# A gather split over five queues: number loads for two chunks at once, sums cleared by transfers, and more columns on ACT

## The chip, the cores and the metric

The kernel runs on one core of a Trainium2 chip. The core has TensorE (PE, with its weight loads PEld), VectorE (DVE), ScalarE (ACT), GpSimd (POOL) and SyncE (SP), each with an instruction queue of its own; SP issues transfers only. The metric is the device time of one execution in microseconds, given as the median of three runs. The profile is that of one more execution.

## The reference

One layer of a graph network over 12,500 nodes and 400,000 edges. Edges are sorted by their target `dst`; the sources `src` are random.

```
h    = max(layernorm(x), 0)                              # 12500 x 48
tmp  = [h[dst], h[src], edge_attr]                       # 400000 x (48+48+32)
msg  = relu(tmp @ W1 + b1) @ W2 + b2
out  = x + segment_sum(msg, dst)                         # 12500 x 48
```

Targets follow a square law (`12500 * u ** 2`), so one edge's target is near the next one's, while each edge needs a row of its own for its source.

## The kernel before

**Tables.** The product with W1 is split in three. Two tables are made first: `tab_a` = h @ W1's first 48 rows + b1, for targets, and `tab_b` = h @ W1's next 48 rows, for sources, both in HBM with 128 numbers a node. `bt` is the second table once more, transposed, in SBUF: 128 partitions, one column of four bytes a node.

**Chunks.** The edges go in 391 chunks of 8 tiles of 128 edges (the last has 5). For chunk c the loop in `windows` (lines 501 to 553) works in three iterations. In iteration c, `prepare` loads the edge attributes (`lhs`), the targets (`row`) and 80 consecutive rows of `tab_a` from the chunk's first target on (`rhs`, whose start is a number in a register); DVE turns targets into a one-hot matrix in `lhs` (L379) and later into its transpose `hot` (L389). In iteration c + 1, `before` puts the target part and the edge part into `pre` with 16 PE instructions (L400), `gathered` adds the source part (L421) and `hidden` applies the relu on ACT (`hid`, L437). In iteration c + 2, `fold` sums the messages by target into `p_g` (L445, L448), and `add` puts these 80 columns into a running window `seg` of sums, on DVE (L460).

**Sources: three ways.** A tile of 128 source rows comes to `gathered` in one of three ways.

- POOL gathers a tile with one indirect transfer from `tab_b` (`gb`, L371). Seven `gb` buffers let it work ahead.
- By columns: DVE and ACT copy single columns of `bt` into a tile `gt` (L348), one instruction an edge, its place in a register. Per chunk 143 columns are copied, 71 by DVE and 72 by ACT, so a tile is full about every 0.9 chunks.
- By rows: SP issues one transfer of 512 bytes an edge from `tab_b` (`gs`, L289), 15 per chunk.

`tiles_of` works out which tile of which chunk comes by columns (430 tiles) and by rows (45); POOL has the remaining 2,618.

**Registers.** Places come into registers by a load on the engine's own queue (`numbers`, L272). `PARTS` lists the groups: (by DVE?, place in the strip of numbers, how many). A group is one load, its size rounded up to a multiple of four, and then its copies. DVE has five groups (8, 15, 16, 20, 12; the second load also brings the place for `add`), ACT has six (12, 8, 8, 20, 12, 12). SP loads the chunk's first target and 15 rows' places, 16 numbers a chunk.

**Order.** It is written out by hand (L501 to L553); each engine follows its own instructions in that order. DVE, in an iteration: one-hot (L379), groups 0 and 1, the segment's output add (L495, when there is one), `add` (L460), the segment change (when there is one), group 2, `hot` (L389), groups 3 and 4. ACT: groups 5 to 7, `hid`, groups 8 to 10. PE: `before`, `fold`, `gathered`. SP: `lhs`, `row`, its load of numbers, `rhs`, the rows, then a segment's load or store. SP's transfers take turns at eight completion semaphores, so an issue also waits until the transfer eight places before it has landed. `lhs` and `row` have three buffers each.

**Segments.** Twelve chunks share one window `seg` of 1,024 targets, in two copies. At the end of a segment (`segment_next`, L471) DVE clears the other copy with two memsets (L476), all but its first 80 columns, and carries the last 80 columns over (L478). In the next segment's first chunks PE multiplies the old window by W2 (`segment_sum`, L484), DVE adds it to x (L495), and in the third chunk SP stores it (L499); before that store SP waits for DVE's add.

Of the kernel before, what the change touches and what calls it, by code (L numbers as in the profile page):

```python
# [16 lines left out]
P = 128  # L17
# [7 lines left out]
NCH = (NT + T - 1) // T  # L25
W = 80
# [4 lines left out]
L = 1024  # L31
# [4 lines left out]
STORE = 2  # L36
# [19 lines left out]
ROWS0 = 3  # L56
# [1 line left out]


PARTS = (  # L60
    (True, 0, 8), (True, 8, 15), (True, 24, 16), (True, 40, 20), (True, 60, 12),
    (False, 72, 12), (False, 84, 8), (False, 92, 8), (False, 100, 20), (False, 120, 12),
    (False, 132, 12),
)
PLACE = 23
STRIP = 144
PART = sum(n for _, _, n in PARTS)
SLOT = [at + k for _, at, n in PARTS for k in range(n)]
FIRST_OF = [sum(n for _, _, n in PARTS[:k]) for k in range(len(PARTS))]
RPART = 15  # L70
BASE = 0

BT0 = 16512
SEG0 = 161696
SEG_SIZE = 8 * L


AT_PLACE, AT_SEG, SEG, NEXT = 16, 17, 18, 19
WIDTH = 20
SLOTS = (NCH + 2 + P - 1) // P  # L80
BANK = 4

# [145 lines left out]


def windows(nc, tc, gp, bt, ident, idx, raw, rhss, x_t, tab_a, tab_b, dst, edge_t, w2s, b2s,  # L230
            sources, out_t):


    srci, rel, bw, wrow, last, cols, degs = idx
# [1 line left out]
    with ExitStack() as es:  # L236
        seg = es.enter_context(tc.tile_pool(name="segs", bufs=1))

        segs = [seg.tile([P, 2, L], F32, name=f"seg{k}") for k in range(2)]
# [19 lines left out]
        st = {}  # L259
        gts = {}  # L260
        gss = {}

        def group(c):

# [5 lines left out]
        def numbers(c, at, n, engine, table=last):  # L270

            return nc.values_load_multi_w_load_instructions(  # L272
                table[c % P : c % P + 1, c // P, at : at + n],
                engines=[engine], min_val=0, max_val=1 << 23,
                skip_runtime_bounds_check_because="numbers of nodes, and what is made of them",
            )[1]
# [73 lines left out]
        def prepare(c):  # L350
            n = min(T, NT - c * T)
            at = c * CE
            lhs = ld.tile([P, CE], F32, name="lhs")
            nc.sync.dma_start(lhs[W:K, : n * P], edge_t[:, at : at + n * P])
            row = ld.tile([W, CE], I16, name="row")
            nc.sync.dma_start(
                row[:, : n * P],
                dst[at : at + n * P].rearrange("(o e) -> o e", o=1).to_broadcast([W, n * P]),
            )
            m = max(0, min(RPART, len(BYROWS) * P - (c - ROWS0) * RPART)) if c >= ROWS0 else 0  # L360
            base, *nodes = numbers(c, BASE, 1 + m, mybir.EngineType.SP)
            rhs = rhss[c % 3]
            base = base.with_bounds(min_val=0, max_val=4 * HID * (N - 1))
            nc.sync.dma_start(
                rhs.bitcast(U8)[:W, :],
                taba8[bass.ds(base, 4 * HID * W)].rearrange("(w h) -> w h", w=W),
            )
            st[c] = dict(n=n, rows=nodes)
            gb = gp.tile([P, T, HID], F32, name="gb") if c >= RAW else None
            for t in range(n - len(COLS_OF.get(c, ())) - (c in BYROWS) if c >= RAW else 0):  # L370
                nc.gpsimd.indirect_dma_start(  # L371
                    out=gb[:, t, :], out_offset=None, in_=tab_b[:, :],
                    in_offset=bass.IndirectOffsetOnAxis(
                        ap=srci[:, c * T + t : c * T + t + 1], axis=0
                    ),
                )

            deg = degs[c % 3]
            nc.vector.tensor_scalar(  # L379
                lhs[:W, : n * P], row[:, : n * P], bw[:, c : c + 1], None,  # L380
                op0=ALU.is_equal, op1=ALU.add, accum_out=deg[:, :1],
            )
            st[c].update(rhs=rhs, lhs=lhs, gb=gb, deg=deg)
# [49 lines left out]
        def hidden(c):  # L433
            s = st[c]
            n = s["n"]
            h = wp.tile([P, T, HID], F32, name="hid")
            nc.scalar.activation(h[:, :n, :], s["pre"][:, :n, :], AF.Relu)  # L437
            s["h"] = h
# [32 lines left out]
        def segment_next(g):  # L471

            old, new = segs[g % 2], segs[(g + 1) % 2]
            if g > 0:
                for k in range(2):
                    nc.vector.memset(new[:, k, W:], 0.0)  # L476
            of, = numbers(begin(g), NEXT, 1, mybir.EngineType.DVE)
            nc.vector.tensor_copy(  # L478
                new[:, :, :W], old[:, :, bass.ds(of.with_bounds(min_val=0, max_val=FAR), W)]
            )  # L480

        sums = []
# [18 lines left out]
        with tc.manual_schedule():  # L501
            for c in range(NCH + 2):
                g, k = group(c - 2)
                if c < NCH:
                    prepare(c)
                    rows(c, st[c].pop("rows"))
                if 0 <= c - 1 < NCH:
                    before(c - 1)
                if 0 <= c - 2 < NCH:
                    fold(c - 2)  # L510
                columns(c, 0)
                columns(c, 1)
                segment_add()
                if 0 <= c - 2 < NCH:
                    add(c - 2)
                    if k == GQ - 1:
                        segment_next(g)
                columns(c, 2)
                if c < NCH:
                    compare(c)  # L520
                if c < 2:
                    nc.vector.memset(segs[c], 0.0)
                columns(c, 3)
                columns(c, 4)
                columns(c, 5)
                columns(c, 6)
                columns(c, 7)
                if 0 <= c - 1 < NCH:
                    gathered(c - 1)
                    hidden(c - 1)  # L530
                columns(c, 8)
                columns(c, 9)
                columns(c, 10)
                if k == GQ - 3 or c == NCH - 1:
                    segment_load(g)
                if g > 0 and k < L // BLK:
                    segment_sum(g - 1, k, BLK)
                if g > 0 and k == STORE:
                    segment_store(g - 1, L)
                if c == NCH + 1:  # L540
                    segment_sum(g, 0, END_L)
                    segment_add()
                    segment_store(g, END_L)
                if c < RAW:
                    raw_turn(c)
                if c == 1:
                    sources()
                for i in range(c * TURNS, min((c + 1) * TURNS, BLOCKS)):
                    turn(i)

                if c < PIECES:
                    s = slice(c * PIECE, (c + 1) * PIECE)
                    nc.sync.dma_start(out_t[:, s], x_t[:, s])  # L553
# [126 lines left out]
def tile_gnn_preln(  # L680
# [13 lines left out]
    places: bass.AP,  # L694
    edge_t: bass.AP,
    ones: bass.AP,
    w1: bass.AP,
    b1: bass.AP,
    w2: bass.AP,
# [10 lines left out]
    nc = tc.nc  # L710
# [39 lines left out]
    with tc.tile_pool(name="keep", bufs=1) as keep, tc.tile_pool(  # L750
# [69 lines left out]
        def check():  # L820

            p_c = ps_c.tile([1, P], F32, name="p_c")
            nc.tensor.transpose(p_c, furthest, ident)
            out_of = keep.tile([1, 1], F32, name="out_of")
            nc.vector.tensor_reduce(out_of, p_c, AX.X, ALU.max)
            nc.vector.tensor_scalar(flag, out_of, 0.5, None, op0=ALU.is_gt)

            nc.vector.tensor_scalar_add(wcol, wcol, -HALF)
            nc.vector.tensor_scalar(bw, b0f[:W, :], wcol[:W, :], None, op0=ALU.add)

            nc.vector.tensor_scalar(cols, cols, 4, BT0, op0=ALU.mult, op1=ALU.add)
            rows_at = slice(BASE, BASE + 1 + RPART)
            nc.vector.tensor_scalar(
                last[:, :, rows_at], last[:, :, rows_at], 4 * HID, None, op0=ALU.mult
            )
            nc.vector.tensor_tensor(
                last[:, :, NEXT : NEXT + 1], last[:, :, NEXT : NEXT + 1],
                last[:, :, SEG : SEG + 1], op=ALU.subtract,
            )
            at = last[:, :, AT_PLACE : AT_PLACE + 1]  # L840
            nc.vector.scalar_tensor_tensor(
                at, last[:, :, AT_SEG : AT_SEG + 1], -4.0, at, op0=ALU.mult, op1=ALU.add
            )
            at_place = slice(PLACE, PLACE + 1)
            nc.vector.scalar_tensor_tensor(
                cols[:, :, at_place], cols[:, :, at_place], 1.0, at, op0=ALU.mult, op1=ALU.add
            )
# [5 lines left out]

    with tc.If(outside == 0) as cmp:
        windows(nc, tc, gp, bt, ident, (srci, rel, bw, wrow, last, cols, degs), (xg, wb, ht), rhss,
                x_t, tab_a, tab_b, dst16, edge_t, w2s, b2s, sources, out_t)
    with cmp.Else():
        general(nc, tc, bt, ident, x_t, tab_a, tab_b, src_it, dst_it, dst, edge_t, w1, w2s, b2s,
                accs, out_t)
# [75 lines left out]
```

## Time and profile before

| | us |
|---|---|
| median of three runs | 3365.4 (3362.72 to 3370.66) |
| profiled execution | 3372.65 |
| its span, first to last instruction | 3370.8 |
| ACT busy | 3035.6 (90%) |
| DVE busy | 2800.1 (83%) |
| PE busy | 2775.6 (82%) |
| POOL busy | 2530.0 (75%) |
| DMA engines busy, after the start | about a third |

The span is the time from the first to the last instruction; the profiled execution's own time lies 1.9 us above it. Busy time counts an engine's datapath. Loads into registers, semaphore waits and the issuing of transfers do not count, so a queue can be full while its engine looks idle: such idle time stands as "issue". Rows with a q behind the engine's name (DVEq, ACTq, SPq) are instructions of the queue itself. A group's row gives busy time and mean duration, then the idle time before it and what ended it; copies follow each other before the last has ended, so their mean is longer than their pitch.

### The profile page before, as it was taken

The page shows a single profiled execution, that of the slowest core. Times are in us where ns is not written, and L with a number is a line of the kernel's source. Part 1 is how long each engine was busy: PE and PEld are TensorE (multiplying, and loading weights), DVE is VectorE, ACT ScalarE, POOL GpSimd, SP SyncE. Part 2 cuts the span into 40 slices and gives each one's busy share as a digit, 9 for nine tenths or more (in the row PEclk, how much of TensorE's full clock was granted, in tenths as well). Part 3 has the DMA queues.
Part 4 walks back from the last instruction along what each step waited for, and adds up shares of the span by engine and source line. Part 5 has one row for each costly group of instructions (what it writes and reads, how often), then busy time and mean ns, then how long its engine had stood idle before and what let it go on. Part 6 is the DMA issues. An engine that isn't in the chain of part 4 may idle for free.

```text
span 3370.8 us, 115212 instructions
## 1 busy us (share of the span) xinstructions
PE 2775.6 (82%) x16394; PEld 2158.3 (64%) x16394; DVE 2800.1 (83%) x29140; ACT 3035.6 (90%) x28179; POOL 2530.0 (75%) x2670
## 2 busy tenths in 40 slices
PE   7987778888888888888887788888788788788777
PEld 6666666666666666666666666676666666666565
DVE  6588888888888888888888888888888888888876
ACT  5799998999998999998899999889998999999987
POOL 7677777777777777777777777777777777777776
PEclk9999998998898998988889999888998999899989
DMA  7433333333333333333333333333333333333333
GB/s 262 122 97 104 100 97 100 99 101 100 100 99 100 95 100 102 100 101 97 100 98 101 100 100 102 95 101 97 102 99 98 97 100 98 104 100 97 99 96 83
DMA packets 200234, 349.24 MB, mean 104 GB/s; under 512 B 69219, under 2 KB 107749, under 8 KB 198181
## 3 DMA queue, kind: packets, MB, share of 16 engines
q0 software_dynamic: 84800, 172.53, 18.9%
q1 hardware_dynamic: 114258, 169.09, 16.7%
q14 instruction: 634, 5.19, 0.5%
q8 instruction: 138, 2.26, 0.3%
q10 hardware_dynamic: 404, 0.17, 0.0%
HBM read 322.05 MB, written 22.07 MB: 102 GB/s over the span
## 4 chain that ended last, share of the span: by engine, by line
DVE 71%; issue 14%; PE 5%; DVEq 4%; POOL 2%; DMA 2%; ACT 0%; SPq 0%; POOLq 0%; ACTq 0%
DVE gt L348 47%; DVE lhs L379 12%; DVE hot L389 8%; DVEq L272 4%; DVE seg L460 2%; POOL gb L371 2%; PE pre L400 1%; PE p_g L445 1%; DVE xseg L495 1%; DVE seg L476 1%; DMA row<-in_dst 1%; PE p_f L488 1%; PE p_f L489 1%; DMA gb<-tab_b,srci 1%; PE p_n L195 1%
## 5 line engine op out<-in xcount | busy, mean ns | idle before, releaser
L371 POOL DMA_INDIRECT gb<-tab_b,srci x2618 | 2489.4, 951 | 812.7 <-issue 724.4
L348 ACT COPY gt<-bt 128x1 f32 x27705 | 2618.0, 188 | 63.9 <-issue 54.6
L348 DVE COPY gt<-bt 128x1 f32 x27335 | 1842.1, 144 | 463.3 <-issue 435.1
L400 PEld LDWEIGHTS pre<-rhs,lhs 112*128 112x128 f32 x6250 | 823.5, 208 | 277.1 <-issue 193.4
L400 PE MATMUL pre<-rhs,lhs 112*128 112x128 f32 x6250 | 841.5, 292 | 98.3 <-issue 56.7
L445 PE MATMUL p_g<-hot,hid 128*128 128x80 f32 x6250 | 794.0, 282 | 131.2 <-ACT hid L437 129.1
L445 PEld LDWEIGHTS p_g<-hot,hid 128*128 128x128 f32 x6250 | 758.4, 198 | 164.4 <-ACT hid L437 161.6
L421 PE MATMUL pre<-gb,ident 128*128 128x512 f32 (+2 forms) x1548 | 771.2, 627 | 34.3 <-DMA gb<-tab_b,srci 26.5
L437 ACT ACTIVATE hid<-pre 128x1024 f32<-128x1024 f32 x391 | 397.5, 1017 | 220.2 <-PE pre L421 205.8
L379 DVE TENSOR_SCALAR_CACHE_REDUCE lhs<-row,bw 80x1024 f32<-80x1024 int16 x391 | 494.6, 1265 | 14.8 <-DMA row<-in_dst 14.5
L421 PEld LDWEIGHTS pre<-gb,ident 128*128 128x128 f32 x1548 | 311.8, 225 | 281.0 <-issue 261.7
L421 PE MATMUL pre<-ident,gt 128*128 128x128 f32 x860 | 214.9, 336 | 261.7 <-DVE gt L348 234.7
L421 PEld LDWEIGHTS pre<-ident,gt 128*128 128x128 f32 x860 | 143.8, 210 | 291.5 <-issue 136.4
L389 DVE TENSOR_TENSOR hot<-wnum,rel 128x640 f32<-128x640 f32 x391 | 318.2, 814 | 0.0
L460 DVE TENSOR_TENSOR seg<-seg,p_g 128x160 f32 x391 | 121.5, 311 | 47.8 <-PE p_g L448 47.8
L448 PE MATMUL p_g<-ident,deg 80*128 80x80 f32 x782 | 156.4, 283 | 0.0
L448 PEld LDWEIGHTS p_g<-ident,deg 80*128 80x128 f32 x782 | 123.6, 198 | 0.0
L488 PE MATMUL p_f<-seg,w2s 128*48 128x512 f32 (+1 forms) x134 | 82.2, 700 | 44.3 <-DVE xseg L495 43.9
L489 PE MATMUL p_f<-seg,b2s 1*48 1x512 f32 (+1 forms) x134 | 76.2, 650 | 0.0
L488 PEld LDWEIGHTS p_f<-seg,w2s 128*48 128x48 f32 x134 | 12.3, 135 | 85.9 <-DVE xseg L495 60.0
L476 DVE MEMSET seg<- 128x944 f32 x64 | 54.1, 845 | 9.3
L489 PEld LDWEIGHTS p_f<-seg,b2s 1*48 1x48 f32 x134 | 11.3, 122 | 65.2 <-issue 65.2
(76 smaller groups left out, 429.0 us busy)
## 6 DMA issues: line engine op xcount, KB each, us to landing
gs<-tab_b SPq DMA_DIRECT2D x5760, 0.5 KB
row<-in_dst SPq DMA_DIRECT2D x390, 160.0 KB
lhs<-in_edge_t SPq DMA_DIRECT2D x390, 128.0 KB
gb<-tab_b,srci POOLq DMA_INDIRECT x2618
rhs<-tab_a SPq DMA_DIRECT2D x391, 40.0 KB
xseg<-in_x_t SPq DMA_DIRECT2D x33, 192.0 KB
out_x<-xseg SPq DMA_DIRECT2D x33, 192.0 KB
tab_b<-tab SPq DMA_DIRECT2D x3, 1280.0 KB
```

Of the source, the lines that this page charges most:

```text
L272: return nc.values_load_multi_w_load_instructions(table[c % P : c % P + 1, c // P, at : at + n], engines=[engine], min_val=0, max_val=1 << 23,
L348: copy(gts[j][:, e : e + 1], bt8[:, bass.ds(of, 4)].bitcast(F32))
L371: nc.gpsimd.indirect_dma_start(out=gb[:, t, :], out_offset=None, in_=tab_b[:, :], in_offset=bass.IndirectOffsetOnAxis(ap=srci[:, c * T + t ...
L379: nc.vector.tensor_scalar(lhs[:W, : n * P], row[:, : n * P], bw[:, c : c + 1], None, op0=ALU.is_equal, op1=ALU.add, accum_out=deg[:, :1],)
L389: nc.vector.tensor_tensor(hot[:, :n, :], wnum.unsqueeze(1).to_broadcast([P, n, W]), rel[:, c * T : c * T + n].unsqueeze(2).to_broadcast([P ...
L400: nc.tensor.matmul(pre[:, t, :], s["lhs"][:K, t * P : (t + 1) * P], s["rhs"][:K, :], start=t % BANK == 0, stop=False, skip_group_check=True,)
L421: nc.tensor.matmul(pre[:, t:e, :], lhsT, rhs, start=False, stop=True, skip_group_check=True)
L437: nc.scalar.activation(h[:, :n, :], s["pre"][:, :n, :], AF.Relu)
L445: nc.tensor.matmul(p_g[:, 0, :], s["h"][:, t, :], s["hot"][:, t, :], start=t == 0, stop=t == n - 1)
L448: nc.tensor.matmul(p_g[:, 1, :], s["deg"], ident[:W, :W], start=True, stop=True)
L460: nc.vector.tensor_add(to, to, s["p_g"])
L488: nc.tensor.matmul(p_f[:, :n], w2s, seg[:, 0, s], start=True, stop=False)
```

## The change

- SP loads numbers for two chunks at once, 32 places in every second chunk, and eight first targets in every eighth. It copies 16 rows a chunk.
- The two memsets of the segment change are gone. A new `segment_clear` clears one eighth of the old window by a transfer from a small array of zeros, in each of eight chunks, the third to the tenth of the next segment. SP issues it at the end of its iteration.
- DVE copies 72 columns in four groups (23, 16, 17, 16) and ACT 76 in five (12, 16, 20, 12, 16). The first group's load has 24 numbers and brings the place for `add`. In DVE's order: one-hot, group 0, `add`, group 1, `hot`, groups 2 and 3. ACT: groups 4 and 5, `hid`, groups 6 to 8.
- With 148 columns and 16 rows a chunk, 445 tiles come by columns and 48 by rows; POOL has 2,600.

```diff
 PARTS = (
-    (True, 0, 8), (True, 8, 15), (True, 24, 16), (True, 40, 20), (True, 60, 12),
-    (False, 72, 12), (False, 84, 8), (False, 92, 8), (False, 100, 20), (False, 120, 12),
-    (False, 132, 12),
+    (True, 0, 23), (True, 24, 16), (True, 40, 17), (True, 60, 16),
+    (False, 76, 12), (False, 88, 16), (False, 104, 20), (False, 124, 12), (False, 136, 16),
 )
 PLACE = 23
-STRIP = 144
+STRIP = 152
...
-RPART = 15
-BASE = 0
+RPART = 16
+BASE, BASES = 2 * RPART, 8
+CLEAR = 8
...
-            base, *nodes = numbers(c, BASE, 1 + m, mybir.EngineType.SP)
+            if c % BASES == 0:
+                bases[:] = numbers(c, BASE, BASES, mybir.EngineType.SP)
+            if c % 2 == 0 and c + 1 >= ROWS0:
+                ahead[:] = numbers(c, 0, 2 * RPART, mybir.EngineType.SP)
+            base, nodes = bases[c % BASES], ahead[c % 2 * RPART :][:m]
...
         def segment_next(g):
 
             old, new = segs[g % 2], segs[(g + 1) % 2]
-            if g > 0:
-                for k in range(2):
-                    nc.vector.memset(new[:, k, W:], 0.0)
             of, = numbers(begin(g), NEXT, 1, mybir.EngineType.DVE)
...
+        def segment_clear(g, k):
+
+            n = 2 * (L - W) // CLEAR
+            half, at = divmod(k, CLEAR // 2)
+            nc.sync.dma_start(
+                segs[g % 2][:, half, W + at * n : W + (at + 1) * n],
+                zeros.unsqueeze(0).to_broadcast([P, n]),
             )
...
                 columns(c, 0)
-                columns(c, 1)
                 segment_add()
                 if 0 <= c - 2 < NCH:
                     add(c - 2)
                     if k == GQ - 1:
                         segment_next(g)
-                columns(c, 2)
+                columns(c, 1)
                 if c < NCH:
                     compare(c)
                 if c < 2:
                     nc.vector.memset(segs[c], 0.0)
+                columns(c, 2)
                 columns(c, 3)
                 columns(c, 4)
                 columns(c, 5)
-                columns(c, 6)
-                columns(c, 7)
                 if 0 <= c - 1 < NCH:
                     gathered(c - 1)
                     hidden(c - 1)
+                columns(c, 6)
+                columns(c, 7)
                 columns(c, 8)
-                columns(c, 9)
-                columns(c, 10)
...
+                if g > 0 and begin(g + 1) < NCH and 0 <= k - STORE < CLEAR:
+                    segment_clear(g - 1, k - STORE)
```

What is left out lays out the arrays of numbers on the host in the new order, hands `zeros` through, and widens the range that is scaled once at the start.

More of the change, by code (lines that the diff above doesn't have):

```diff
@@ L69 @@
 FIRST_OF = [sum(n for _, _, n in PARTS[:k]) for k in range(len(PARTS))]
-RPART = 15
-BASE = 0
+RPART = 16
+BASE, BASES = 2 * RPART, 8
+CLEAR = 8
 BT0 = 16512
-SEG0 = 161696
+SEG0 = 162208
 SEG_SIZE = 8 * L
-AT_PLACE, AT_SEG, SEG, NEXT = 16, 17, 18, 19
-WIDTH = 20
+AT_PLACE, AT_SEG, SEG, NEXT = 40, 41, 42, 43
+WIDTH = 44
 SLOTS = (NCH + 2 + P - 1) // P
@@ L230, in windows @@
 def windows(nc, tc, gp, bt, ident, idx, raw, rhss, x_t, tab_a, tab_b, dst, edge_t, w2s, b2s,
-            sources, out_t):
+            zeros, sources, out_t):
     srci, rel, bw, wrow, last, cols, degs = idx
@@ L261, in windows @@
         gss = {}
+        bases, ahead = [], []
         def group(c):
@@ L479, in segment_next @@
                 new[:, :, :W], old[:, :, bass.ds(of.with_bounds(min_val=0, max_val=FAR), W)]
+            )
+        def segment_clear(g, k):
[4 more added lines that the diff above has]
+                zeros.unsqueeze(0).to_broadcast([P, n]),
             )
@@ L696, in tile_gnn_preln @@
     ones: bass.AP,
+    zeros: bass.AP,
     w1: bass.AP,
@@ L831, in check @@
             nc.vector.tensor_scalar(cols, cols, 4, BT0, op0=ALU.mult, op1=ALU.add)
-            rows_at = slice(BASE, BASE + 1 + RPART)
+            rows_at = slice(0, BASE + BASES)
             nc.vector.tensor_scalar(
@@ L855, in tile_gnn_preln @@
         windows(nc, tc, gp, bt, ident, (srci, rel, bw, wrow, last, cols, degs), (xg, wb, ht), rhss,
-                x_t, tab_a, tab_b, dst16, edge_t, w2s, b2s, sources, out_t)
+                x_t, tab_a, tab_b, dst16, edge_t, w2s, b2s, zeros, sources, out_t)
     with cmp.Else():
@@ L883 @@
     numbers[2 : NCH + 2, AT_PLACE] = SEG0 + of % 2 * SEG_SIZE - BT0
-    numbers[:NCH, BASE] = first
+    bases = np.pad(first, (0, -NCH % BASES)).reshape(-1, BASES)
+    numbers[: len(bases) * BASES : BASES, BASE : BASE + BASES] = bases
     numbers[:NCH, SEG] = seg
@@ L895 @@
     rows = by_tile[in_rows].reshape(-1)
-    rows = np.pad(rows, (0, -len(rows) % RPART)).reshape(-1, RPART)
-    numbers[ROWS0 : ROWS0 + len(rows), BASE + 1 : BASE + 1 + RPART] = rows
+    by_chunk = np.zeros((NCH + NCH % 2) * RPART, np.int32)
+    by_chunk[ROWS0 * RPART : ROWS0 * RPART + len(rows)] = rows
+    numbers[: NCH + NCH % 2 : 2, : 2 * RPART] = by_chunk.reshape(-1, 2 * RPART)
     last = np.ascontiguousarray(numbers.reshape(SLOTS, P, WIDTH).transpose(1, 0, 2))
@@ L919 @@
         "ones": np.ones((1, NR // 2 * P), np.float32),
+        "zeros": np.zeros(2 * (L - W) // CLEAR, np.float32),
         "w1": np.asarray(L0_gnn_W1),
```

## The prediction

> **What bounds the kernel now.** First the page: span, busy shares, the gathers.
>
> ```profile
> span 3370.8 us, 115212 instructions
> PE 2775.6 (82%) x16394; PEld 2158.3 (64%) x16394; DVE 2800.1 (83%) x29140; ACT 3035.6 (90%) x28179; POOL 2530.0 (75%) x2670
> L371 POOL DMA_INDIRECT gb<-tab_b,srci x2618 | 2489.4, 951 | 812.7 <-issue 724.4 <-DMA gb<-tab_b,srci 45.5 <-PE pre L421 29.4
> ```
>
> No engine looks full. Next, the busy time by window (500 to 2900 us): of the gathers (L371), then of the one ACT instruction per chunk (L437).
>
> ```profile
> 500.00:2900.00 2400.00, 1816.87 (x1912) 0.90 0.36 99
> 500.00:2900.00 2400.00, 291.95 (x287) 0.90 0.36 99
> ```
>
> A gather takes 2400/1912 = 1.255 us with the gap behind it, so POOL is full without looking it; a chunk takes 2400/287 = 8.36 us. POOL would need (8 - 143/128 - 15/128) x 1.255 = 8.49 us per chunk: it is living off the lead that seven gb buffers gave it at the start. What sets 8.36? DVE's waits, then one of its chunks in order of time, and the register loads (L272) on its queue in that chunk, taken window by window.
>
> ```profile
> DVE gt L348 <- issue: 435.1, 1272, 1.2
> DVE lhs L379 <- DMA row<-in_dst: 14.5, 7, 7.7
> ```
>
> ```profile
> 1509.83 1.28 DVE L379 TENSOR_SCALAR_CACHE_REDUCE lhs<-row,bw 80x1024 f32<-80x1024 int16 x1
> 1512.02 1.00 DVE L348 COPY gt<-bt 128x1 f32 x15 [0.42 <-issue]
> 1512.94 0.31 DVE L460 TENSOR_TENSOR seg<-seg,p_g 128x160 f32 x1
> 1513.78 1.06 DVE L348 COPY gt<-bt 128x1 f32 x16 [0.52 <-issue]
> 1514.76 0.81 DVE L389 TENSOR_TENSOR hot<-wnum,rel 128x640 f32<-128x640 f32 x1
> 1515.76 1.30 DVE L348 COPY gt<-bt 128x1 f32 x20 [0.19 <-issue]
> ```
>
> ```profile
> L272 DVEq TENSOR_LOAD <-cols x1: 605/605/605, 1509.9 to 1509.9; - x1
> L272 DVEq TENSOR_LOAD <-cols x1: 1115/1115/1115, 1510.8 to 1510.8; - x1
> L272 DVEq TENSOR_LOAD <-cols x1: 1114/1114/1114, 1512.6 to 1512.6; - x1
> L272 DVEq TENSOR_LOAD <-cols x1: 1379/1379/1379, 1514.3 to 1514.3; - x1
> L272 DVEq TENSOR_LOAD <-cols x1: 851/851/851, 1516.4 to 1516.4; - x1
> L272 DVEq TENSOR_LOAD <-cols x1: 616/616/616, 1517.8 to 1517.8; - x1
> ```
>
> The loads carry 8, 16, 16, 20 and 12 numbers. From the first to the next chunk's first is 7.9 us, of which they take 605 + 1115 + 1114 + 1379 + 851 = 5064 ns; the other 2.8 us issue 71 copies and three larger instructions. DVE's queue is never free, and nearly all idle time of its datapath is "issue", hardly any a wait for data. So DVE's issuing bounds the loop, not its copying: an ordinary chunk is worth what its loads and issues add up to.
>
> **The change part by part: DVE.** A load costs 605 ns for 8 numbers and 1379 for 20, so 64.5 per number and 89 for the load itself. The four new loads carry 24, 16, 20 (17 rounded up to fours) and 16: 1637 + 1115 + 1379 + 1115 = 5246 ns, 182 more than now, since five numbers more are bought for one load less. Issue: after the 20-number load 0.7 us pass until the next (1514.3 + 1.4 to 1516.4), after the 8-number one 0.3, some 0.03 per copy and 0.06 per group. One copy more and one group less give -0.03. That is +0.15 us per chunk. Above it lies a full queue: when the 851 ns load starts at 1516.4, of 20 copies issued some ten have begun (0.062 us each from 1515.76), so ten stand ahead. A group of 23 would run past ten, and its last copies would issue at the datapath's 0.062: +0.1 at most, none if the queue is longer. I take +0.18 for both, between 0.12 and 0.25.
>
> Against it stand the memsets. First the chunk that has them, then their group.
>
> ```profile
> 3343.64 0.31 DVE L460 TENSOR_TENSOR seg<-seg,p_g 128x160 f32 x1
> 3344.10 1.83 DVE L476 MEMSET seg<- 128x944 f32 x2
> 3346.91 0.81 DVE L389 TENSOR_TENSOR hot<-wnum,rel 128x640 f32<-128x640 f32 x1
> L476 DVE MEMSET seg<- x64: 845/845/845, 225.6 to 3345.1; 128x944 f32 x64
> L272 DVEq TENSOR_LOAD <-last x33: 303/314/545, 125.8 to 3343.7; - x33
> ```
>
> From add to compare it is 3.27 us here and 1.82 in the chunk above: 1.45 for the segment change. The copy of 80 columns stays with its own load (0.31) and issue, and during the memsets the queue ran ahead, which shortens what follows. The saving lies between 0.4 and 1.1; I take 0.7, times 32 pairs. The first and last memset give the segment: (3345.1 - 1 - 225.6)/31 = 100.6 us for 12 chunks. DVE's segment becomes 100.6 + 12 x 0.18 - 0.7 = 102.1 (101.0 to 103.2).
>
> **ACT.** One chunk, and loads of 8 and of 20 numbers:
>
> ```profile
> 1513.64 1.01 ACT L437 ACTIVATE hid<-pre 128x1024 f32<-128x1024 f32 x1
> 1514.55 6.75 ACT L348 COPY gt<-bt 128x1 f32 x72
> 1521.59 1.02 ACT L437 ACTIVATE hid<-pre 128x1024 f32<-128x1024 f32 x1 [0.28 <-PE pre L421]
> L272 ACTq TENSOR_LOAD <-cols x1: 553/553/553, 1511.2 to 1511.2; - x1
> L272 ACTq TENSOR_LOAD <-cols x1: 1263/1263/1263, 1513.2 to 1513.2; - x1
> ```
>
> A copy takes 6.75/72 = 0.094 us, four more cost 0.375 per chunk. Without its wait the cycle is 7.67, so 8.04 after. All 72 ran without a gap: their loads hide behind queued copies. The two new loads of 16 take 1.03 (59 ns a number); ten queued copies cover 0.94 of it. So 8.1, at most 8.4 if the cover is smaller, 97 to 101 us a segment: ACT's slack is nearly used, and a late hid delays PE's fold, then DVE's add.
>
> [...]
>
> **SP.** Its waits at the store (500 to 3000 us), one of its chunks, its loads, and two 128-row transfers of the start:
>
> ```profile
> SPq L499 <- DVE seg L460: 102.6, 17, 10.3
> SPq L499 <- DVE xseg L495: 50.7, 8, 9.2
> 1571.15 0.33 SPq L354 DMA_DIRECT2D lhs<-in_edge_t  x1
> 1573.72 4.81 SPq L289 DMA_DIRECT2D gs<-tab_b  x15
> 1578.64 0.33 SPq L354 DMA_DIRECT2D lhs<-in_edge_t  x1
> L272 SPq TENSOR_LOAD <-last x459: 274/1186/1317, 75.8 to 3363.4; - x153
> 7.99 0.42 SPq L768 DMA_DIRECT2D b0f<-in_first_f  x1
> 9.44 0.93 SPq L771 DMA_DIRECT2D cols<-in_src_strip  x1
> ```
>
> SP's chunk is 7.49 us. Its only real slack is the wait before a store, 153.3 us in 2500/100.6 = 24.9 segments: 6.2 us each. Per segment the change adds: 12 row copies at 4.81/15 = 0.32, +3.8; loads of 32 in six chunks (1186 + 16 x 61 = 2162 ns) for 16 in twelve, with 0.06 around each, -1.6; one and a half loads of eight bases, +1.0; eight clears at 0.42 to 0.93 and 0.05 around, +3.8 to +7.8, likelier the low end, which is also a broadcast to 128 partitions. Odd chunks have no load between the row transfer and the row copies, so a transfer slot is wanted back about 1.2 us sooner; bounds 0 and 0.3 each, +0 to +1.8. Sum +7.0 to +12.8; I take 8.4, so 100.6 + 8.4 - 6.2 = 102.8 (101.4 to 107.2). Behind a clear wait the next chunk's lhs and row transfers, and behind the row transfer DVE's first instruction.
>
> **POOL** is relieved of 18 tiles (15 from columns, 3 from rows): 18 x 1.255 = 22.6 us, worth that only where POOL ends last. That is so near the end:
>
> ```profile
> PE pre L421 <- DMA gb<-tab_b,srci: 26.5, 19, 2.8
> ```
>
> (waits from 2900 us on). The gain is 0 to 26; I take 5, as PE has slack before DVE. Initial loads are wider by 8 and 24 columns: under 1 us.
>
> **The sum.** Three queues end near 102 us per segment; the slowest, SP, is taken: +2.2 x 32 segments = +70, less 5: span 3436. The profiled execution took 3372.65 around its span of 3370.8, the median 3365.4, 5.4 below that span: 3430.
>
> **The rivals.** (1) DVE sets the pace and SP stays inside its slack: clears at 0.42, no slot waits, ACT's loads covered. The segment grows by 12 x 0.15 - 0.7 = 1.1, or 0.7 to 1.5: 3382 to 3408. For it: SP's low end is only 0.8 over its present slack.
>
> (2) Faster: dropping a load saves a fixed time on DVE's queue, and merging 8 and 16 numbers into 24 costs less than the sum. Were 0.4 us saved per chunk, the loop would fall to 8.0, under POOL's (8 - 148/128 - 16/128) x 1.255 = 8.43; POOL would run end to end and the run would lose its 22.6 us: 3343. It decides from about 0.15 saved per chunk. Against it: the four sizes lie on one line with only 89 ns of intercept, and one number alone takes 314. For it: no load of 24 stands in this trace.
>
> [...]
>
> (3) Clears near 0.93, or rows landing behind them: SP's segment over 104.5, above 3490, up to 3570 at the upper bound.
>
> **How the numbers follow.** Issuing with SP at the edge, 3408 to 3490: 0.48. DVE alone, 3382 to 3408: 0.25. Worse: 0.09. Within 0.2%, 3359 to 3372 (a measurement of this kernel tells no less than 0.2%): 0.04. Faster: 0.14. The range 3360 to 3490 leaves out the faster case and the worst; the likeliest one's own range is 3408 to 3490. Slower has 0.48 + 0.25 + 0.09 = 0.82.
>
> **What would show it.** DVE: loads of about 1640 ns, no memsets, more "issue" per chunk although there is a load less. SP: waits at the store near nothing, row waits of DVE above 14.5 us, clears of 0.4 to 0.5. ACT: gaps in its 76 copies ahead of the 16-number loads. POOL: 2600 gathers, more waits for free buffers. The prediction is wrong if the load of 24 costs under 1.3 us, or if the segment, from one seg copy (L478) to the next, is below 100.6.

## The result: 7% slower, and the profile after

The changed kernel takes 3602.2 us (median of four runs, 3600.7 to 3607.0) where the kernel before takes 3367.3 on the same chip: 1.070 times as long, 95% interval 1.068 to 1.072. That is 235 us more, beyond the upper end of the range. The page's span, gathers and chain of the changed kernel:

```profile
span 3599.8 us, 117642 instructions
PE 2893.5 (80%) x16430; PEld 2241.7 (62%) x16430; DVE 2784.2 (77%) x29461; ACT 3240.1 (90%) x29714; POOL 2494.3 (69%) x2652
DVE 24%; SPq 19%; PE 14%; DMA 13%; issue 12%; ACT 10%; POOL 5%; DVEq 2%; ACTq 1%; POOLq 0%
L376 POOL DMA_INDIRECT gb<-tab_b,srci x2600 | 2453.2, 944 | 1032.0 <-issue 727.0
```

Busy shares again name no culprit. The chain does: SP's queue (19%) and transfers (13%) stand on it. In the chain of the kernel before, DVE had 71% and both of these next to nothing:

```profile
DVE 71%; issue 14%; PE 5%; DVEq 4%; POOL 2%; DMA 2%; ACT 0%; SPq 0%; POOLq 0%; ACTq 0%
```

One row gives the segment, the unit of everything below: the copy of 80 columns, once a segment, 33 times. Before, then after (line, count, durations, first and last start):

```profile
L478 DVE COPY seg<-seg x33: 177/179/244, 126.3 to 3345.8; 128x160 f32 x33
```

```profile
L480 DVE COPY seg<-seg x33: 243/245/388, 126.6 to 3574.5; 128x160 f32 x33
```

(3345.8 - 126.3)/32 = 100.61 us before, (3574.5 - 126.6)/32 = 107.75 after. 32 segments of 7.14 more are 228 of the 229 us between the two spans: the loss is inside the loop.

Next the waits of SP's own queue. The columns are total us, times, longest:

```profile
SPq L290 <- DMA lhs<-in_edge_t: 60.3, 100, 2.1
SPq L290 <- DMA seg<-in_zeros: 51.5, 87, 1.7
SPq L510 <- DVE seg L465: 41.7, 22, 7.6
SPq L510 <- DVE xseg L506: 40.4, 12, 29.9
SPq L290 <- DMA row<-in_dst: 32.3, 87, 1.2
```

Before, the two waits at the store (L499 there) came to 153 + 82 us and stood first, and the row copies hardly waited for a transfer slot. After, the waits at the store (L510) are 82 us, and the row copies (L290) wait 144 us for `lhs`, a clear or `row` to land, because these hold the slots they want. SP has become the longest queue. Its order in time shows where the wait sits:

```profile
1505.03 2.49 SPq L290 DMA_DIRECT2D gs<-tab_b  x8
1507.57 0.36 SPq L488 DMA_DIRECT2D seg<-in_zeros  x1
1508.04 0.36 SPq L355 DMA_DIRECT2D lhs<-in_edge_t  x1
1508.46 0.41 SPq L357 DMA_DIRECT2D row<-in_dst  x1
1508.96 0.38 SPq L369 DMA_DIRECT2D rhs<-tab_a  x1
1509.43 7.08 SPq L290 DMA_DIRECT2D gs<-tab_b  x16
...
1518.67 0.41 SPq L357 DMA_DIRECT2D row<-in_dst  x1
1521.70 0.33 SPq L369 DMA_DIRECT2D rhs<-tab_a  x1
1522.13 0.93 SPq L290 DMA_DIRECT2D gs<-tab_b  x3
```

Three copies take 0.93 and eight 2.49, so sixteen would take about 5.0; here they take 7.08. This is a chunk without a load of numbers (nothing between `row` and `rhs`; in the next chunk 3.03 us lie there). The fifth copy wants the slot of the clear, eight transfers back, 3.2 us after its issue, and just finds it free; the sixth waits 1.15 us for that of `lhs`, the seventh 0.47 for that of `row`.

DVE then waits for its rows, and POOL for buffers that PE gives back late:

```profile
POOL gb L376 <- PE pre L426: 264.2, 136, 13.9
DVE lhs L384 <- DMA row<-in_dst: 103.3, 121, 8.7
ACT gt L349 <- issue: 78.9, 254, 0.8
DVE gt L349 <- issue: 590.7, 1326, 1.4
```

Before, the first was 29.4 us in 51 waits, the second 14.5 in 7, the third 54.6 and the last 435.1. So the named waits for rows are less than half of DVE's loss. Its "issue" grew too, and no run splits what of that follows from a late row.

The packet records say how late. Median from SP's issue of a transfer to the end of its last packet, in us, here with three experiments told below:

| | before | after | `late` | `apart` | `narrow` |
|---|---|---|---|---|---|
| `lhs` | 1.73 | 2.62 | 1.73 | 1.85 | 1.77 |
| `row` | 2.59 | 3.10 | 2.60 | 2.74 | 2.59 |
| a clear | | 3.02 | 3.18 | 1.85 | 1.36 |

The changed kernel holds its own comparison: between 500 and 3000 us `lhs` lands in 2.91 us right behind a clear and in 1.78 in the chunks without one, `row` in 3.37 and 2.53.

### The profile page after: what moved, and what is told of

The parts are those of the page before. It is cut to its first block, busy times and chain, and to the rows that moved or that the text cites. A ratio compares the mean times of both kernels' runs of the same rounds, so it can differ in the third digit from the quotient of the medians.

```text
span 3599.8 us, 117642 instructions
## 1 busy us (share of the span) xinstructions
PE 2893.5 (80%) x16430; PEld 2241.7 (62%) x16430; DVE 2784.2 (77%) x29461; ACT 3240.1 (90%) x29714; POOL 2494.3 (69%) x2652
## 4 chain that ended last, share of the span: by engine, by line
DVE 24%; SPq 19%; PE 14%; DMA 13%; issue 12%; ACT 10%; POOL 5%; DVEq 2%; ACTq 1%; POOLq 0%
DVE gt L349 15%; SPq L290 10%; ACT gt L349 9%; DMA row<-in_dst 8%; PE pre L426 5%; DVE lhs L384 4%; PE pre L405 4%; SPq L273 4%; POOL gb L376 4%; DVE hot L394 2%; DMA rhs<-tab_a 2%; PE p_g L450 2%; SPq L355 2%; DVEq L273 2%; DMA gb<-tab_b,srci 1%
## 5 line engine op out<-in xcount | busy, mean ns | idle before, releaser
L376 POOL DMA_INDIRECT gb<-tab_b,srci x2600 | 2453.2, 944 | 1032.0 <-issue 727.0
L349 ACT COPY gt<-bt 128x1 f32 x29240 | 2825.7, 187 | 122.4 <-issue 78.9
L405 PEld LDWEIGHTS pre<-rhs,lhs 112*128 112x128 f32 x6250 | 842.7, 212 | 303.4 <-issue 225.4
L405 PE MATMUL pre<-rhs,lhs 112*128 112x128 f32 x6250 | 860.7, 296 | 114.4 <-DVE lhs L384 69.2
L450 PE MATMUL p_g<-hot,hid 128*128 128x80 f32 x6250 | 816.6, 287 | 167.4 <-ACT hid L442 166.6
L450 PEld LDWEIGHTS p_g<-hot,hid 128*128 128x128 f32 x6250 | 780.4, 203 | 200.3 <-ACT hid L442 198.8
L426 PE MATMUL pre<-gb,ident 128*128 128x512 f32 (+2 forms) x1548 | 810.7, 657 | 0.0
L426 PE MATMUL pre<-ident,gt 128*128 128x128 f32 x890 | 236.1, 355 | 366.9 <-DVE gt L349 301.3
L426 PEld LDWEIGHTS pre<-gb,ident 128*128 128x128 f32 x1548 | 333.7, 239 | 259.5 <-issue 233.5
L499 PE MATMUL p_f<-seg,w2s 128*48 128x512 f32 (+1 forms) x134 | 86.3, 732 | 31.6 <-DVE xseg L506 31.1
L499 PEld LDWEIGHTS p_f<-seg,w2s 128*48 128x48 f32 x134 | 12.4, 136 | 73.4 <-DVE xseg L506 45.2
L506 DVE TENSOR_TENSOR xseg<-xseg,p_f 48x512 f32<-48x512 f32 (+1 forms) x67 | 44.7, 667 | 6.9 <-PE p_f L500 6.9
```

The source lines that it names most:

```text
L349: copy(gts[j][:, e : e + 1], bt8[:, bass.ds(of, 4)].bitcast(F32))
L376: nc.gpsimd.indirect_dma_start(out=gb[:, t, :], out_offset=None, in_=tab_b[:, :], in_offset=bass.IndirectOffsetOnAxis(ap=srci[:, c * T + t ...
L405: nc.tensor.matmul(pre[:, t, :], s["lhs"][:K, t * P : (t + 1) * P], s["rhs"][:K, :], start=t % BANK == 0, stop=False, skip_group_check=True,)
L426: nc.tensor.matmul(pre[:, t:e, :], lhsT, rhs, start=False, stop=True, skip_group_check=True)
L450: nc.tensor.matmul(p_g[:, 0, :], s["h"][:, t, :], s["hot"][:, t, :], start=t == 0, stop=t == n - 1)
```

## The experiments

All ratios are against the kernel before on the same chip, timed in the same batch; times are medians. Segments come from the copy's row, as above.

**Which part costs it.** The theory: SP's queue is now the longest, because of the clears. First, the clears are taken out of the changed kernel and the memsets put back.

```diff
+            if g > 0:
+                for k in range(2):
+                    nc.vector.memset(new[:, k, W:], 0.0)
...
-                if g > 0 and begin(g + 1) < NCH and 0 <= k - STORE < CLEAR:
-                    segment_clear(g - 1, k - STORE)
```

> The changed kernel with the two memsets of the segment change back on DVE and no clears by transfers; all else as changed. Theory S (SP's queue sets the pace, and most of its extra time comes from the clears: their issue, 8 x 0.46 us a segment, and the waits for transfer slots behind them, 5.2 us a segment): SP's work per segment falls from 106.6 to about 97.7 us, DVE's issuing takes over, 3400 to 3430 us where the kernel before takes 3365. Rival R (the 16th row and the paired loads of numbers are what SP cannot bear): above 3520 us. Rival C (the column groups on DVE and ACT set the pace): above 3550.

```profile
DVE 53%; ACT 21%; issue 13%; PE 5%; POOL 3%; DVEq 3%; ACTq 1%; DMA 1%; POOLq 0%; SPq 0%
L483 DVE COPY seg<-seg x33: 173/179/243, 127.0 to 3391.9; 128x160 f32 x33
```

3433.3 us, ratio 1.020 (1.018 to 1.021), 3 us above the range; the trace is of its fastest run, 3419.3, with a segment of 102.03. SP is off the chain. So inside the change, clears in place of memsets cost 3602 - 3433 = 169 us. This is a net figure: the run without clears pays for its memsets.

Then each part alone, in the kernel before. The clears in place of the memsets, nothing else:

> The kernel before with the clears by transfers in place of the memsets, nothing else. Theory S: SP had 6.2 us of slack a segment; the clears take 3.7 us of issue, and since each chunk still has its load of numbers between the row transfer and the row copies, the slot waits come to 0 to 2.5 us: SP stays just inside, 3350 to 3390 us. Rival T (the clears' transfers alone delay lhs and row so much that DVE waits, whatever SP's work): above 3440 us.

```profile
DVE 35%; PE 17%; SPq 14%; issue 12%; DMA 11%; ACT 5%; DVEq 3%; POOL 1%; ACTq 0%
L476 DVE COPY seg<-seg x33: 243/245/397, 127.1 to 3425.1; 128x160 f32 x33
```

3452.9, ratio 1.025 (1.023 to 1.027): the theory that eight clears alone fit into SP's slack was wrong, and the time lies where rival T put it, above 3440. The trace of it has SP's waits at the store down from 6.2 to 3.0 us a segment, so slack was left; yet DVE waits 59 us for rows instead of 14.5, most of it in the chunks right behind the segment's store and behind its load of x, where SP comes late. That a clear delays `row` further there, and that slack elsewhere in the segment does not help, is argued from these places.

The new groups of columns alone (`PARTS` and the order):

> The kernel before with the new column groups alone (72 by DVE in four loads, 76 by ACT in five), SP and the memsets as before. Theory D (DVE's issuing: 182 ns more of loads a chunk, and a group of 23 that runs into the full queue, 0.2 us a chunk): 3420 to 3450 us. Rival 2 of the prediction (a load less is a saving): POOL ends last, about 3343 us. Columns free of charge: 3355 to 3370 us.

```profile
DVE 55%; ACT 19%; issue 13%; PE 7%; DVEq 3%; POOL 2%; ACTq 1%; DMA 1%; SPq 0%
L477 DVE COPY seg<-seg x33: 175/179/244, 128.1 to 3397.3; 128x160 f32 x33
```

3425.1, ratio 1.018 (1.016 to 1.020), as expected. DVE's ordinary chunk, 8.11 to 8.19 us before, now takes 8.29 to 8.37.

SP's new loads and its sixteenth row alone:

> The kernel before with SP's part alone: numbers of two chunks in one load, bases of eight chunks in one, 16 rows a chunk; columns and memsets as before. Theory S: SP's work per segment rises by 3.9 us for the rows, falls by 0.6 for the loads, and 0 to 1.8 of slot waits come in odd chunks; 95 + 3 to 5 is inside 100.6: 3355 to 3375 us. Rival R: above 3420 us.

```profile
L484 DVE COPY seg<-seg x33: 175/179/244, 128.8 to 3359.7; 128x160 f32 x33
```

3387.6, ratio 1.005 (1.004 to 1.007): a little above the range; SP's wait at the store falls to 1.0 us a segment, so the slack is nearly used up by this alone.

The three parts alone cost 85 + 57 + 20 = 162 us; together 235. The excess comes with the clears: columns and rows together (`no_clears`) cost 66 us, less than their 77 apart, while the clears cost 85 alone and 169 beside the other two. Clears and rows spend the same 6.2 us of SP's slack, which is there once. The columns do not: in `columns_only` SP waits 7.5 us a segment at the store.

**What about a clear costs so much.** Three causes were open: SP's time to issue it, the delay of what stands behind it, and the way it reads, 128 pieces of 944 bytes from one and the same address. The first experiment clears 16 partitions instead of 128:

```diff
-                segs[g % 2][:, half, W + at * n : W + (at + 1) * n],
-                zeros.unsqueeze(0).to_broadcast([P, n]),
+                segs[g % 2][:16, half, W + at * n : W + (at + 1) * n],
+                zeros.unsqueeze(0).to_broadcast([16, n]),
```

> The changed kernel with each clear on 16 partitions in place of 128: as many issues, an eighth of the bytes (so the sums of the other partitions are not cleared, and the output is not the reference's). Theory S1 (what the clears cost beyond their issue is their data, ahead of lhs and row in the same rings): lhs and row land as without clears, SP's slot waits fall from 5.7 to about 2.7 us a segment, SP's work from 106.6 to 103.2, 3470 to 3500 us. Rival S2 (the issues alone fill SP): 3570 or above.

```profile
L488 SPq DMA_DIRECT2D seg<-in_zeros x256: 326/327/1016, 155.0 to 3422.1; - x128
L480 DVE COPY seg<-seg x33: 243/245/494, 128.4 to 3443.9; 128x160 f32 x33
```

3469.3, ratio 1.031 (1.028 to 1.033). The other partitions keep their old sums. SP issues as many clears as the changed kernel and each in nearly the same time, yet 133 of the 169 us are gone. There the row is:

```profile
L488 SPq DMA_DIRECT2D seg<-in_zeros x256: 362/366/427, 153.2 to 3552.5; - x128
```

The 256 more transfers of SP explain the 36 us that are left above `no_clears`, and what that run pays for its memsets (0.7 us a segment by the section on them, some 22 us, an estimate).

The second issues the clear behind the next chunk's `lhs` and `row` instead of ahead of them:

```diff
-        bases, ahead = [], []
+        bases, ahead, late = [], [], []
...
+            while late:
+                segment_clear(*late.pop())
...
-                    segment_clear(g - 1, k - STORE)
+                    late.append((g - 1, k - STORE))
```

> The changed kernel with each clear issued behind the next chunk's lhs and row transfers in place of ahead of them; as many issues and bytes. Theory S1 (lhs and row land late, 3.0 to 3.7 us in place of 1.8 and 2.5, since the clear's data are ahead of them): they land as without clears, DVE's waits for row (103 us) go, slot waits fall for lhs and come for the clear itself; 3480 to 3550 us. Rival S2 (place is of no account, SP's count of work is): 3590 to 3610.

```profile
SPq L290 <- DMA seg<-in_zeros: 65.4, 91, 1.6
SPq L290 <- DMA row<-in_dst: 28.7, 62, 1.6
```

```profile
DVE lhs L386 <- DMA row<-in_dst: 71.9, 71, 7.9
```

3530.1, ratio 1.048 (1.046 to 1.050), inside the range. `lhs` and `row` land as in the kernel before (the table), and SP's wait for `lhs`' slot falls from 60.3 to 4.5 us; the edit is worth 72 us. The row copies now wait for the clear itself, which is no faster (3.18 us). DVE's waits for rows were expected to go; 72 of 103 us stay.

The third leaves order and size, and gives every partition zeros of its own to read:

```diff
-                zeros.unsqueeze(0).to_broadcast([P, n]),
+                zeros,
...
-        "zeros": np.zeros(2 * (L - W) // CLEAR, np.float32),
+        "zeros": np.zeros((P, 2 * (L - W) // CLEAR), np.float32),
```

> The changed kernel with the zeros read from 128 rows of their own in place of one row of 944 bytes read 128 times. Theory H (the one row in HBM is read by all engines at once and that makes the clear slow, 3.0 us): the clear lands in under 2.5 us and the time falls by 30 us or more. Theory S1 as it stands (128 pieces of 944 bytes take that long from anywhere): 3595 to 3610 us.

```profile
SPq L290 <- DMA row<-in_dst: 40.8, 97, 2.0
SPq L290 <- DMA lhs<-in_edge_t: 10.8, 22, 1.1
```

```profile
L488 SPq DMA_DIRECT2D seg<-in_zeros x256: 362/366/1117, 153.6 to 3441.9; - x128
L480 DVE COPY seg<-seg x33: 243/244/435, 127.0 to 3463.6; 128x160 f32 x33
```

3503.7, ratio 1.041 (1.039 to 1.043): 98 us faster than the change with the same number of pieces, bytes and issues (366 ns each, as before). The clear lands in 1.85 us instead of 3.02, the wait for its slot falls from 51.5 to 2.6 us and that for `lhs` from 60.3 to 10.8.

TensorE's granted clock, 0.91 before and 0.88 after, does not explain these differences: the profiles of `no_clears`, `narrow`, `apart` and `late` have 0.887 to 0.891, and their times lie between 3433 and 3530.

So the 169 us go in three steps: 98 for reading one row 128 times (3602 to 3504), 35 for moving 128 pieces instead of 16 (to 3469), 36 for the issues and slots, less the memsets (to 3433). The first step is one edit; the other two differ in more than one thing, so their names are argued. The runs of `apart` lie between 3490.6 and 3508.2, so the first two steps are known to some 10 us.

**What bounded the kernel before.** If DVE alone did, four columns moved from DVE to ACT would free 4 x 64.5 ns of loads and 4 x 0.03 of issue per chunk.

```diff
-    (True, 0, 8), (True, 8, 15), (True, 24, 16), (True, 40, 20), (True, 60, 12),
-    (False, 72, 12), (False, 84, 8), (False, 92, 8), (False, 100, 20), (False, 120, 12),
+    (True, 0, 8), (True, 8, 15), (True, 24, 16), (True, 40, 16), (True, 56, 12),
+    (False, 68, 12), (False, 80, 12), (False, 92, 8), (False, 100, 20), (False, 120, 12),
```

> The kernel before with four columns moved from DVE to ACT: DVE's group of 20 becomes 16, ACT's first group of 8 becomes 12; still 143 columns a chunk, and the same tiles by each way. Theory D (DVE's issuing sets the pace before): DVE's chunk loses 4 x (64 + 31) = 380 ns, ACT's gains 4 x 93 = 370 and stays under 8.2; POOL, full at 1.255 us a gather, sets the pace: 3340 to 3355 us. Rival (POOL or ACT sets the pace already): 3365 us or above.

```profile
ACT 45%; POOL 18%; PE 17%; issue 10%; ACTq 4%; DMA 4%; DVE 1%; SPq 0%; DVEq 0%; POOLq 0%
```

```profile
L371 POOL DMA_INDIRECT gb<-tab_b,srci x2618: 940/944/1921, 52.4 to 3346.1; - x187
```

In the kernel before:

```profile
L371 POOL DMA_INDIRECT gb<-tab_b,srci x2618: 940/947/1924, 52.6 to 3353.5; - x187
```

3363.2, ratio 0.9988 (0.9978 to 0.9998): not the expected gain. DVE's share of the chain goes from 71% to 1%, and ACT and POOL take its place. POOL's 2,618 gathers run from 52.4 to 3346.1, 1.259 us each, with only 28 us of waits for buffers in all; shifting columns between DVE and ACT can hardly end the loop before them. In the kernel before they end only 7 us later. So DVE bounded the kernel before by little more than these 6 us; ACT and POOL stood right behind it.

**The same edits on other chips.** Eight earlier runs landed on two chips where the kernel before takes 5324 and 5329 us. A kernel that is bound otherwise there cannot test reasons read from a trace of 3371 us, so all five edits were tried again, above. What was expected, with the result behind each, as ratio to the kernel before on that chip. Without the clears, twice:

> The changed kernel with the two memsets of the segment change back on DVE and no clears by transfers; all else as changed. Theory S (SP's queue sets the pace, and most of its extra time comes from the clears: their issue, 8 x 0.46 us, and the waits for transfer slots behind them, 5.2 us a segment): SP's work per segment falls from 106.6 to about 97.7 us, DVE's issuing takes over, 3400 to 3430 us. Rival R (the 16th row and the paired loads of numbers are what SP cannot bear): the time stays above 3520 us. Rival C (the column groups on DVE and ACT set the pace): the time stays above 3550.

> The changed kernel with the two memsets of the segment change back on DVE and no clears by transfers; all else as changed. Theory S (SP's queue sets the pace, and most of its extra time comes from the clears: their issue, 8 x 0.46 us a segment, and the waits for transfer slots behind them, 5.2 us a segment): SP's work per segment falls from 106.6 to about 97.7 us, DVE's issuing takes over, 3400 to 3430 us where the kernel before takes 3365. Rival R (the 16th row and the paired loads of numbers are what SP cannot bear): above 3520 us. Rival C (the column groups on DVE and ACT set the pace): above 3550.

5436.6 and 5444.4 us, 1.022 both (1.018 to 1.025, 1.020 to 1.024). Clears alone, twice:

> The kernel before with the clears by transfers in place of the memsets, nothing else. Theory S: SP had 6.2 us of slack a segment; the clears take 3.7 us of issue, and since each chunk still has its load of numbers between the row transfer and the row copies, the slot waits come to 0 to 2.5 us: SP stays just inside, 3350 to 3390 us. Rival T (the clears' transfers alone delay lhs and row so much that DVE waits, whatever SP's work): above 3440 us.

> The kernel before with the clears by transfers in place of the memsets, nothing else. Theory S: SP had 6.2 us of slack a segment; the clears take 3.7 us of issue, and since each chunk still has its load of numbers between the row transfer and the row copies, the slot waits come to 0 to 2.5 us: SP stays just inside, 3350 to 3390 us. Rival T (the clears' transfers alone delay lhs and row so much that DVE waits, whatever SP's work): above 3440 us.

5353.8 and 5352.1, 1.005 and 1.004. Columns alone, twice:

> The kernel before with the new column groups alone (72 by DVE in four loads, 76 by ACT in five), SP and the memsets as before. Theory D (DVE's issuing: 182 ns more of loads a chunk, and a group of 23 that runs into the full queue, 0.2 us a chunk): 3420 to 3450 us. Rival 2 of the prediction (a load less is a saving): POOL ends last, about 3343 us. Theory S alone, with columns free: 3355 to 3370 us.

> The kernel before with the new column groups alone (72 by DVE in four loads, 76 by ACT in five), SP and the memsets as before. Theory D (DVE's issuing: 182 ns more of loads a chunk, and a group of 23 that runs into the full queue, 0.2 us a chunk): 3420 to 3450 us. Rival 2 of the prediction (a load less is a saving): POOL ends last, about 3343 us. Columns free of charge: 3355 to 3370 us.

5428.3 and 5426.4, 1.019 and 1.018. Rows alone:

> The kernel before with SP's part alone: numbers of two chunks in one load, bases of eight chunks in one, 16 rows a chunk; columns and memsets as before. Theory S: SP's work per segment rises by 3.9 for the rows, falls by 0.6 for the loads, and 0 to 1.8 of slot waits come in odd chunks; 95 + 3 to 5 us is inside 100.6: 3355 to 3375 us. Rival R: above 3420 us.

5346.7, 1.003 (1.002 to 1.005). Four columns moved:

> The kernel before with four columns moved from DVE to ACT: DVE's group of 20 becomes 16, ACT's first group of 8 becomes 12; still 143 columns a chunk, and the same tiles by each way. Theory D (DVE's issuing sets the pace before): DVE's chunk loses 4 x (64 + 31) = 380 ns, ACT's gains 4 x 93 = 370 and stays under 8.2; POOL, full at 1.255 us a gather, sets the pace: 3340 to 3355 us. Rival (POOL or ACT sets the pace already): 3365 us or above.

5433.8, 1.020 (1.018 to 1.022). In microseconds none of these was expected, since none of the expectations knew the chip. Nothing on the change is concluded from them; what such a chip shows of itself stands at the end.

## Why the prediction was wrong

The direction was right, and the queue that the sum took as the slowest, SP, did come to stand on the chain. The size was wrong, in SP's term; 3602 lies above even the upper end of rival 3.

**SP's sum (the failed step).** It took 8.4 us of added work a segment, less 6.2 of slack: +2.2. From SP's instructions between 500 and 3000 us, per segment of each kernel (a wait is the gap ahead of an instruction beyond its usual one):

| | before | after | difference | taken |
|---|---|---|---|---|
| row copies, issue and register move | 46.96 | 49.86 | +2.9 (and gaps) | +3.8 |
| loads | 15.13 | 14.42 | -0.7 | -0.6 |
| clears, issue | | 2.97 | +3.0 (and gaps) | +3.8 |
| `lhs`, `row`, `rhs`, issue | 13.79 | 14.74 | +1.0 | 0 |
| gaps between instructions | 15.92 | 17.15 | +1.2 | in the rows |
| row copies' waits for a slot | 1.15 | 5.79 | +4.6 | +1.4 (0 to 1.8) |
| wait at the store | 5.98 | 1.10 | -4.9 | -6.2 |

The work that SP itself does was priced well: loads, copies and clears (0.37 us each, the low end) make +6.4 with their gaps, against +7.0. Two things failed. The slot waits are +4.6 where 1.8 was the bound: that bound came from transfers that land as fast as before, and a clear takes 3.0 us to land and delays `lhs` from 1.73 to 2.62. (`rows_only`, without a clear, has 3.0 us of slot waits, about 1.8 more than before: SP's own part alone reaches the bound, and the rest comes with the clears.) And the slack was not used to the end: 1.1 us of it remain while DVE waits for rows elsewhere in the segment. The slack lies in one place, before the store, and the clears stand in the eight chunks behind it; that this is the reason is argued. A smaller miss is the issue of `lhs`, `row` and `rhs`, put at nothing: +1.0. Net +7.1 instead of +2.2.

**"Behind a clear wait lhs and row".** The prediction saw the place and gave it no price in the sum; it was left to rival 3 at 9%. The row it priced a clear by was the issue of a 128-row transfer, and issue was the smaller part: `narrow` and `apart` show 133 us that lie in how a clear reads and lands, with the issue time as it was or nearly so. Rival 3's first half (clears at 0.93) is refuted; its second half came true.

**DVE's loads and groups.** The load of 24 was to take 1637 ns, the four loads 5246. One chunk after, and the same load in another:

```profile
L273 DVEq TENSOR_LOAD <-cols x1: 1595/1595/1595, 947.8 to 947.8; - x1
L273 DVEq TENSOR_LOAD <-cols x1: 1101/1101/1101, 950.3 to 950.3; - x1
L273 DVEq TENSOR_LOAD <-cols x1: 1350/1350/1350, 952.0 to 952.0; - x1
L273 DVEq TENSOR_LOAD <-cols x1: 1096/1096/1096, 954.0 to 954.0; - x1
L273 DVEq TENSOR_LOAD <-cols x1: 1677/1677/1677, 1503.8 to 1503.8; - x1
```

Loads of one size differ by up to 5% between these two chunks; the median of the 24s is about 1640. +0.18 per chunk is what `columns_only` shows. Its segment grew by 1.55 us, not 12 x 0.18 = 2.2, as the chunk with the store shrank by 0.5. Rival 2, that a load less saves a fixed time, is refuted: the line of 64.5 ns a number held beyond its last point (it gives 1637 for 24). The load of 24 in place of 8 and 16 saved about 80 ns (605 + 1115 against 1640), and the four loads as a whole saved none (1595 + 1101 + 1350 + 1096 = 5142 ns in the first chunk above, against 5064 for the five before).

**The memsets.** From add to compare the segment change takes this long after:

```profile
1534.62 0.31 DVE L465 TENSOR_TENSOR seg<-seg,p_g 128x160 f32 x1
1534.96 0.24 DVE L480 COPY seg<-seg 128x160 f32 x1
1536.15 1.06 DVE L349 COPY gt<-bt 128x1 f32 x16 [0.95 <-issue]
1537.13 0.81 DVE L394 TENSOR_TENSOR hot<-wnum,rel 128x640 f32<-128x640 f32 x1
```

2.51 us, where it was 3.27 with the memsets. `clears_only`, with the old groups around it, has 2.56 in the median of 33: 0.71 saved, the 0.7 taken. Over the whole chunk it is 0.6: the chunk of the change exceeds its neighbours by 0.6 us there, by 1.2 before. What it was worth at the end of the run, where DVE no longer set the pace alone, no run separates.

**Rival 1 (DVE alone, 3382 to 3408)** failed because SP did not stay inside its slack. Its price for DVE was sound: `columns_only`, at 3425, still has the memsets, and less 32 x 0.7 us it would come to 3403 (an estimate).

**ACT.** Its copies show gaps now and then, as foretold (254 of 0.3 us in the mean, 157 before), and "issue" rose from 55 to 79 us: hidden here. But its cycle of 8.04, or 8.4 at most, with 76 copies was too low. ACT's wait for PE between 500 and 3000 us, before and in `columns_only`:

```profile
ACT hid L437 <- PE pre L421: 153.6, 95, 8.5
ACT hid L436 <- PE pre L420: 12.5, 19, 2.6
```

That is 0.5 us of a segment of 102.16, so ACT alone needs about 8.47 us a chunk with the new groups. DVE waits for data 0.1 us a segment there. So DVE is the tighter of the two, but only by some 0.4 us a segment; that freeing DVE alone could hardly have gained anything is argued from this.

**POOL.** 2,600 gathers, as foretold, and waits for buffers of 264 us instead of 29: the 22.6 us of gathers saved bought nothing. The remark that POOL is full was right for the kernel before: `moved` shows POOL as the next floor there.

**The list of signs.** Loads, gathers, more "issue" on DVE and row waits came as listed. A clear's issue took 0.37 us, a little under the 0.4 to 0.5 listed. "Waits at the store near nothing" came only by two thirds (235 to 82 us over the run).

## What to carry to other kernels

Work moved to the queue that issues transfers cost more than its issue here (the clears' issue was 3.0 us a segment, and the slot waits grew by 4.6): ask when the new transfer lands, which completion slot it holds until then, and which later transfer of the same queue is wanted soonest; price it at landing, not at issue. A source that is broadcast from one small row to 128 partitions was no cheap read here (3.02 us to land, 1.85 from 128 rows): give each partition its own bytes, or clear on an engine. Slack that lies at one point of a period is spent once, and work that stands behind that point may not reach it (here 1.1 us of SP's were left).

## What was not expected of the hardware

- **One row read by many pieces was slow.** Same pieces, bytes and issue time (128 of 944 bytes, 366 ns): 3.02 us to land from one row of 944 bytes, 1.85 from 128 rows, and transfers behind it are late too (`lhs` 2.62 against 1.85). Why is not shown. The kernel has another read of this kind, `row`, 80 pieces from one row of 2 KB, for which DVE's first instruction waits; no run gives it rows of its own.
- **Chips on which three queues stall together.** On the two chips with 5324 and 5329 us for the kernel before, the granted clock was 0.73 instead of 0.91. Had the whole time grown as the clock fell, it would be 1.25 times as long (an estimate); it was 1.58 times. The waits of `clears_alone` there:

```profile
DVE gt L349 <- issue: 2069.6, 3437, 1.6
ACT gt L349 <- issue: 1719.3, 2822, 1.2
```

DVE's 515 us of "issue" in `clears_only` are 2070 there, ACT's 59 are 1719, though they load and copy the same numbers. In order of time DVE, ACT and SP stop for 0.5 us or more after every one to three copies and go on at the same moments, and run undisturbed for a few us between: DVE starts again at 1500.71, 1502.17, 1503.57, 1510.00 and 1511.42 us, ACT at 1500.72, 1502.14, 1503.57, 1509.98 and 1511.41, and SP issues at 1500.00, 1501.42, 1502.86 and 1503.57. What stops them stays open.
